# Down projection of a pair of tiles as seven products of two by two blocks, its bias as a matmul row, turned probabilities in place

## The chip, the core and the metric

The kernel runs on one core of a Trainium2 chip. The core has five engines that run side by side: TensorE (PE, with PEld for its weight loads), VectorE (DVE), ScalarE (ACT), GpSimd (POOL) and SyncE (SP, which issues most of the DMAs). Each takes its instructions in order and waits at semaphores for the others. SBUF is the on-chip memory, PSUM the memory that TensorE writes; this kernel uses PSUM as banks of 512 f32 columns. The metric is the device time of one execution in microseconds. All data and all matmuls are f32, unless said otherwise.

## What is computed

For x of 4096 tokens with 256 features the reference computes `x + attention_block(xn) + expert_block(xn)`, with xn the layer norm of x:

```python
# attention block: 8 heads, windows of 64 tokens, keys of the window before, the own and the next, band of 64
scores = einsum("bhcqd,bhckd->bhcqk", q, k3) * scale          # masked to the band
o = einsum("bhcqk,bhckd->bhcqd", softmax(scores), v3)
x = layernorm(x + o @ Wo + bo) * gamma + beta
x = x + gelu(x @ W1 + b1) @ W2 + b2
# expert block: 8 experts, two for each token, weights comb from the softmax of the gate's logits
h = silu((xf @ gw.T + gb) * (xf @ uw.T + ub))                 # 816 hidden columns
y = sum over experts of comb[:, e] * (h @ dw.T + db)
```

The change is in `h @ dw.T + db`, the down projection of the experts, and in how the probabilities of the attention are kept.

## The kernel before

**Units.** The tokens of each expert are gathered into tiles of 128. A unit is a pair of tiles (256 tokens) or a single tile of one expert. Thirty-four units always run: thirty pairs, with singles as units 3, 7, 11 and 15. Five more run only where the routing needs them; these go through `whole`, and the change leaves their down projection as it is.

**A step.** A loop over b = 0 to 33 does, in one step, gate and up of unit b, down of unit b-1 and, for b below 32 (`STEPS`), the attention of two tiles of queries (i, i+1) and one half of the heads (hq). An even b has hq 0. The order on every engine is that of the program (`manual_schedule`): nothing is reordered later. In a step TensorE does, in this order: the scores; the rest part of down (`down_rest`, L908); chunks 0 and 1 of gate/up; in even steps the output projection of the two tiles before (`closing`); the main part of down (`results`, L891); the transposes of the next unit's tokens (`turned`); up to b = 16 one share of keys, values or queries for later tiles; chunk 2; the transposes of the first half of the probabilities (`flip`, L1018, tile pT); chunk 3; those of the second half; two transposes for the keys that two tiles have in common (`flip_rest`, L1031, tile pX); chunk 4; the rest of gate/up; chunk 5; the products of probabilities and values (`weigh`, L1040).

**The probabilities.** VectorE reduces the scores against the mask into `pr` (L962). ScalarE takes the exponentials (L977). GpSimd, for each of four heads, adds the two halves of `pr` (L989) and multiplies the second half with an identity (L990); `apart` (L997) has it prepare `xd` before. In `scale`, VectorE takes the reciprocal of the sums (L1007), scales the first halves (L1009, waits for the last L989), reduces the second halves (L1010, waits for the last L990) and multiplies the result (L1011), for which GpSimd's L1013 waits. After `flip`, two VectorE operations (L1022) multiply the turned probabilities with a mask each, the first into a buffer of its own (`prT`), the second into the free half of `pr`.

**The experts' hidden columns.** 816 columns are six chunks of 128 (`FCM`) and 48 more (`REM`). A chunk is four matmuls, a ScalarE operation for the gate (L841) and a VectorE operation (L842) into `hT`, 128 hidden columns by tokens; silu (L874) follows for two chunks at a time. The 48 columns of the pair's first tile stand in rows 0 to 47 of chunk 6, those of the second in rows 64 to 111; the other rows of chunk 6 are zero.

**Down.** For each tile one matmul over the rows of chunk 6 (L884) and six over the chunks (L895), each of 128 hidden columns with 256 output columns, sum into one PSUM bank per tile (pe). VectorE then adds the bias, which the DMA of the weights `wd` has brought once per partition (256 columns), and writes y (L905); SP stores y (L918), and behind it in SP's queue issue the next loads of `wd` and, later, `wg`.

**Banks.** Seven banks of PSUM are handed out in the order of the program; a matmul into a new bank waits for whoever last read it.

Of the kernel before, what the change touches and what calls it, by code (L numbers as in the profile page):

```python
# [32 lines left out]
F32 = mybir.dt.float32  # L33
# [3 lines left out]
ALU = mybir.AluOpType  # L37
# [4 lines left out]
P = 128  # L42
# [12 lines left out]

REM = FE % P
REM_UP = P // 2
FM = FE - REM  # L60
FCM = FM // P
NT = S // P
G = 512
NG = S // G
# [24 lines left out]

GW, UW, RW, BW = 0, DC * FM, 2 * DC * FM, 2 * DC * FM + DC * P  # L90
GU = BW + 2 * FCM + 1
DN = FCE * D + D
HQ = 4
AHEAD = 4
WARM = 56
# [6 lines left out]
def block_kernel(ctx: ExitStack, tc: tile.TileContext, a: dict, out: bass.AP):  # L102
# [116 lines left out]

    att = ctx.enter_context(ExitStack())  # L220
    wqkv = pool(att, "wqkv", right)
    mask = wqkv.tile([P, 4, 2 * P], F32, tag="mask", name="mask")

# [87 lines left out]
    def make_mask():  # L311

        nc.gpsimd.memset(mask, 0.0)
        for kind in range(4):

            def keep(base, step, channel, m=mask[:, kind, :]):
                nc.gpsimd.affine_select(
                    out=m,  # L320
                    in_=m,
                    compare_op=ALU.is_ge,
                    fill=MASKED,
                    base=base,
                    pattern=[[step, 2 * P]],
                    channel_multiplier=channel,
                )

            keep(0, 1, -1)
            keep(2 * WIN, -1, 1)  # L330
            if kind == 0:
                keep(-WIN, 1, 0)
            if kind == 3:
# [539 lines left out]
    def silu(hT, lo, hi, on=slice(0, P)):  # L873
        nc.scalar.activation(hT[on, lo:hi, :], hT[on, lo:hi, :], AF.Silu)  # L874

    def silu_rest(hT):

        silu(hT, FCM, FCE, slice(0, REM_UP + REM if hT.shape[2] > P else REM))

    def results_rest(pds, w, hT):  # L880
        for t, pd in enumerate(pds):

            half = slice(t * REM_UP, (t + 1) * REM_UP) if len(pds) > 1 else slice(0, P)
            nc.tensor.matmul(  # L884
                pd,
                hT[half, FCM, t * P : (t + 1) * P],
                w[half, FCM * D : FCE * D],
                start=True,
                stop=False,
            )  # L890

    def results(pds, w, hT):
        for t, pd in enumerate(pds):
            for f in range(FCM):
                nc.tensor.matmul(  # L895
                    pd,
                    hT[:, f, t * P : (t + 1) * P],
                    w[:, f * D : (f + 1) * D],
                    start=False,
                    stop=(f == FCM - 1),  # L900
                )

    def summed(y, pds, w):
        for t, pd in enumerate(pds):
            nc.vector.tensor_tensor(y[:, t, :], pd, w[:, FCE * D :], ALU.add)  # L905
# [7 lines left out]
    def down(b, pds, w, hT):  # L913
        at, n, _ = UNITS[b]
        results(pds, w, hT)
        y = he.tile([P, TB, D], F32, tag="y", name=f"y{b}")[:, 0:n, :]
        summed(y, pds, w)
        nc.sync.dma_start(out=rows(done, at, n), in_=y)  # L918

    def whole(b, w, wd, xT, hT, banks, gss, y):  # L920

        _, n, _ = UNITS[b]
        n_in = n * P
        for k, f in enumerate([FCM] + list(range(FCM))):
            pb = halves(banks[k % 3])[:, :, 0:n_in]
            gs = gss[k % 3][:, 0:n_in]
            if f == FCM:
                rest_of(w, xT, hT, pb, gs)
            else:
# [8 lines left out]
        summed(y, pds, wd)  # L938

    def scores(i, hq):  # L940

        g = i // TG
        ps = [halves(bank(f"ps{i}_{hq}_{hh}")) for hh in range(HQ)]
        for j in range(2):
            lo = (i + j) % TG * P
            for hh in range(HQ):
                r = slice(hh * DH, (hh + 1) * DH)
                nc.tensor.matmul(  # L948
                    ps[hh][:, j, :],
                    qts[g][r, hq, lo : lo + P],  # L950
                    kts[g][r, hq, lo : lo + 2 * P],
                    start=True,
                    stop=True,
                )
        kind = 0 if i == 0 else 2 if i == NT - 2 else 1
        pr = sp.tile([P, HQ, 2, 2 * P], F32, tag="pr", name=f"pr{i}_{hq}", bufs=1)

        nm = sp.tile([P, 2, HQ], F32, tag="nm", name=f"nm{i}_{hq}")
        sums = sp.tile([P, 2, HQ], F32, tag="sums", name=f"sums{i}_{hq}")
        for hh in range(HQ):  # L960
            for j in range(2):
                nc.vector.tensor_tensor_reduce(  # L962
                    out=pr[:, hh, j, :],
                    in0=ps[hh][:, j, :],
                    in1=mask[:, kind + j, :],
                    scale=-1.0,
                    scalar=-LOWEST,
                    op0=ALU.add,
                    op1=ALU.min,
                    accum_out=nm[:, j, hh : hh + 1],  # L970
                )
        return pr, nm, sums
# [42 lines left out]
    def flip(i, hq, j, pr):  # L1015
        pb = bank(f"pT{i}_{hq}_{j}")
        for hh in range(HQ):
            nc.tensor.transpose(pb[:, hh * P : (hh + 1) * P], pr[:, hh, j, 0:P], ident)  # L1018

        prT = [sp.tile([P, HQ, P], F32, tag="prT", name=f"prT{i}_{hq}_{j}"), pr[:, :, j, P:]]  # L1020
        for t, m in zip(prT, (first_keys, second_keys)):
            nc.vector.tensor_tensor(  # L1022
                t, pb.rearrange("p (h q) -> p h q", h=HQ), bcast(m, HQ, 1), ALU.mult
            )
        return prT
# [204 lines left out]
    hTs = [he.tile([P, FCE, B], F32, tag=f"hT{k}", name=f"hT{k}", bufs=1) for k in range(2)]  # L1230
    for k in range(2):
        nc.gpsimd.memset(hTs[k][:, FCM, :], 0.0)
    res = {0: residual(0)}
    xT = {}
    pos, oTs = {}, {}
# [11 lines left out]
    for b in range(ALWAYS):  # L1247
# [7 lines left out]

        if b + 2 < ALWAYS:
            xs[b + 2] = gather(b + 2)
        if attends:
            pr, nm, sums = scores(i, hq)
            xd = apart(i, hq)  # L1260
        if 0 < b < STEPS:
            pds = down_rest(b - 1, downs[b - 1], hTs[(b - 1) % 2])
        if b == 0:
            xT[0] = turned(0, xs.pop(0))
        if attends:
            exps(pr, nm, sums, 0, 3)
            merge(pr, 0)
        chunk(0)
        if b >= STEPS:
            pds = down_rest(b - 1, downs[b - 1], hTs[(b - 1) % 2])  # L1270
            down(b - 1, pds, downs.pop(b - 1), hTs[(b - 1) % 2])
        if attends:
            exps(pr, nm, sums, 3, 6)
            merge(pr, 1)
# [5 lines left out]
        if hq == 0 and i - 2 in res:  # L1280
            closing(i - 2, oTs.pop(i - 2), res.pop(i - 2))
            if i < STEPS:
                res[i] = residual(i)
        if attends:
            scale(i, hq, pr, sums, xd)
        if b == STEPS:
# [16 lines left out]
        if b == STEPS + 1:  # L1303
# [2 lines left out]
            nc.vector.scalar_tensor_tensor(shift2, mv2[:, :, 0], -1.0, r2, ALU.mult, ALU.mult)  # L1306
            nc.vector.tensor_tensor(beta_b2, beta, b2, ALU.add)
            x2s[0] = second_loads(0)
        if 0 < b < STEPS:
            down(b - 1, pds, downs.pop(b - 1), hTs[(b - 1) % 2])  # L1310
        if b == ALWAYS - 1:
            load_unit(ALWAYS + 1)
        if b + 1 < ALWAYS:
# [58 lines left out]
    down(ALWAYS - 1, pds, downs.pop(ALWAYS - 1), last)  # L1372
    load_unit(ALWAYS + 2)
    for b in range(ALWAYS, BLOCKS):
        at, n, _ = UNITS[b]
# [139 lines left out]
```

## Time and profile before

| | |
|---|---|
| Time, median of 3 runs | 1083.43 us (1083.07 to 1084.13) |
| The profiled execution, its time | 1085.82 us |
| The same, span of its instructions | 1084.0 us |
| Granted TensorE clock, mean | 0.996 |
| Step of b = 17 (455.15 to 476.00) | 20.85 us: PE busy 20.85, DVE 13.25, ACT 12.25, POOL 10.14 |
| Step of b = 18 (476.00 to 498.58) | 22.58 us: PE busy 22.58, DVE 14.99, ACT 12.25, POOL 11.42 |
| Step of b = 11 (326.83 to 345.70) | 18.87 us: PE busy 18.87, DVE 13.06, ACT 10.33, POOL 10.15 |
| Seven products of the last stage (920.40 to 932.90) | 12.50 us: PE busy 12.50, DVE 8.42, ACT 3.40, POOL 0.12 |

The last four rows are busy times of each engine in a stretch of the span. An engine that is busy for the whole of a stretch doesn't wait in it. In lines of the time line, the first column is the start in microseconds from the span's start, the second the time of the group, then engine, line, operation, what it writes and reads, and how often; in brackets stands the idle time just before, with what ended it. Lines by group give the mean of one in nanoseconds; a matmul of f32 has two records, and the mean of a record is longer than the distance from one to the next, since matmuls are pipelined.

The steps are very regular. The first score matmuls of b = 17 to 31 follow each other by 20.85 us (odd b) and 22.58 us (even b), within 0.01, but for the last.

### The profile page before, as it was taken

How to read it: one execution, taken by the hardware profiler on the slowest of the kernel's cores; microseconds unless marked ns; L12 is line 12 of the kernel's file. 1: busy time of each engine (PE TensorE's matmuls, PEld its weight loads, DVE VectorE, ACT ScalarE, POOL GpSimd, SP SyncE). 2: the span in 40 equal slices, each digit the busy share in tenths (PEclk: the TensorE clock that was granted, in tenths of full speed). 3: DMA queues.
4: the chain of work that ended last, by engine and by line, in shares of the span. 5: the costliest groups of instructions: out<-in, count | busy, mean ns of one | idle time of the engine just before them, and what ended most of it. 6: DMA issues, size and time to landing. Idle time of an engine off the chain costs nothing. (4 is left out here: it accounts for less than half of the span.)

```text
span 1084.0 us, 19063 instructions
## 1 busy us (share of the span) xinstructions
PE 1071.3 (99%) x6808; PEld 858.0 (79%) x6808; DVE 656.5 (61%) x1707; ACT 527.0 (49%) x1226; POOL 452.7 (42%) x600
## 2 busy tenths in 40 slices
PE   8999999999999999999999999999999999999998
PEld 5677888887888788888888888888887847777778
DVE  6565657667666666766666766666533355555546
ACT  3536546555556545655565465556424363333320
POOL 5515544346444554455445544544520043222220
PEclk8999999999999999999999999999999999999999
DMA  8252435454445344644554445445576443333121
GB/s 284 74 204 84 161 128 190 138 186 147 147 163 184 134 150 153 214 147 139 183 185 143 164 158 190 157 135 187 163 246 229 157 146 110 97 98 96 60 63 40
DMA packets 61040, 163.42 MB, mean 151 GB/s; under 512 B 6576, under 2 KB 46896, under 8 KB 51472
## 3 DMA queue, kind: packets, MB, share of 16 engines
q1 hardware_dynamic: 54464, 144.48, 38.1%
q0 software_dynamic: 6480, 17.70, 6.0%
q8 instruction: 55, 0.90, 0.3%
q14 instruction: 41, 0.34, 0.1%
HBM read 140.28 MB, written 21.89 MB: 150 GB/s over the span
## 5 line engine op out<-in xcount | busy, mean ns | idle before, releaser
L833 PE MATMUL gu<-xsT,wg 128*128 128x256 f32 (+1 forms) x1632 | 362.5, 369 | 0.7 <-ACT xsT L825 0.7
L833 PEld LDWEIGHTS gu<-xsT,wg 128*128 128x128 f32 x1632 | 289.1, 190 | 45.3 <-DVE nm L962 8.6
L841 ACT ACTIVATE gs<-gu,wg 128x256 f32<-128x256 f32 (+1 forms) x204 | 92.4, 453 | 256.2 <-PE gu L833 253.3
L842 DVE SCALAR_TENSOR_TENSOR hT<-gu,wg,gs 128x256 f32<-128x256 f32 (+1 forms) x204 | 95.1, 467 | 174.2 <-ACT gs L841 174.0
L989 POOL TENSOR_TENSOR pr<-pr 128x256 f32<-128x256 f32 x128 | 93.0, 727 | 252.5 <-ACT pr L977 252.5
L895 PE MATMUL pe<-wd,hT 128*128 128x256 f32 x768 | 171.6, 379 | 0.0
L895 PEld LDWEIGHTS pe<-wd,hT 128*128 128x128 f32 x768 | 145.4, 190 | 20.5 <-issue 1.0
L1160 POOL DMA_INDIRECT got<-done,slot x64 | 64.3, 1004 | 176.9 <-DVE acc L1173 110.5
L990 POOL TENSOR_TENSOR pr<-pr,ident 128x256 f32<-128x256 f32 x128 | 126.2, 986 | 10.0
L977 ACT ACTIVATE pr<-pr,nm 128x256 f32<-128x256 f32 x256 | 126.7, 497 | 0.4
L1115 PE MATMUL ph<-x2T,W 128*128 128x512 f32 x256 | 111.4, 593 | 1.1 <-ACT x2T L1105 1.1
L962 DVE CUSTOM_DVE_ANT_0 pr<-ps,mask 128x256 f32<-128x256 f32 x256 | 90.7, 420 | 24.3 <-PE ps L948 24.3
L1122 ACT ACTIVATE hf<-ph,b 128x512 f32<-128x512 f32 x64 | 43.4, 688 | 118.3 <-issue 54.6
L874 ACT ACTIVATE hT<-hT 128x512 f32<-128x512 f32 (+3 forms) x148 | 80.8, 546 | 32.1 <-DVE hT L842 22.4
L1115 PEld LDWEIGHTS ph<-x2T,W 128*128 128x128 f32 x256 | 48.0, 190 | 58.9 <-issue 53.3
L807 POOL DMA_INDIRECT xs<-xnd,token x71 | 68.8, 969 | 49.7 <-DVE paired_tiles L774 32.3
L1009 DVE TENSOR_TENSOR pr<-pr,rec 128x1024 f32<-128x1024 f32 x32 | 39.2, 1225 | 27.5 <-POOL pr L989 27.5
L1196 DVE TENSOR_TENSOR acc<-u,acc 128x256 f32<-128x256 f32 x32 | 12.9, 423 | 70.1 <-ACT u L1199 69.6
L977 ACT ACT_TABLE_LOAD x31 | 39.8, 1283 | 23.5 <-DVE nm L962 23.4
L1010 DVE TENSOR_REDUCE same<-pr 128x8 f32<-128x1024 f32 x32 | 39.1, 1222 | 19.8 <-POOL pr L990 19.8
L977 ACT ACTIVATION_READ_ACCUMULATOR pr<-pr,nm 128x1 f32 x256 | 48.4, 189 | 0.0
L1186 PE MATMUL s<-V,hv 128*128 128x128 f32 x384 | 44.2, 275 | 0.0
(230 smaller groups left out, 1575.8 us busy)
## 6 DMA issues: line engine op xcount, KB each, us to landing
wg<-in_gate_up SPq DMA_DIRECT2D x37, 1670.5 KB, 7.0
wd<-in_down SPq DMA_DIRECT2D x37, 1024.0 KB, 5.6
done<-y SPq DMA_DIRECT2D x30, 256.0 KB, 2.2
x<-in_x SPq DMA_DIRECT2D x8, 512.0 KB, 5.4
xnd<-xn SPq DMA_DIRECT2D x8, 512.0 KB, 4.8
res<-xnd SPq DMA_DIRECT2D x16, 256.0 KB, 2.9
x1d<-res SPq DMA_DIRECT2D x16, 256.0 KB, 2.2
x<-x1d SPq DMA_DIRECT2D x8, 512.0 KB, 4.7
```

The lines of the kernel that those rows point to most:

```text
L807: nc.gpsimd.indirect_dma_start(out=x[:, t, :], out_offset=None, in_=xnd, in_offset=bass.IndirectOffsetOnAxis(ap=token[:, i : i + 1], axis=0),)
L833: nc.tensor.matmul(pb[:, k, :], w[:, lo : lo + P], xT[:, c, :], start=(c == 0), stop=(c == DC - 1),)
L841: nc.scalar.activation(gs, pb[:, 0, :], AF.Identity, bias=w[:, gb : gb + 1])
L842: nc.vector.scalar_tensor_tensor(hT[:, f, :], pb[:, 1, :], w[:, ub : ub + 1], gs, ALU.add, ALU.mult)
L874: nc.scalar.activation(hT[on, lo:hi, :], hT[on, lo:hi, :], AF.Silu)
L895: nc.tensor.matmul(pd, hT[:, f, t * P : (t + 1) * P], w[:, f * D : (f + 1) * D], start=False, stop=(f == FCM - 1),)
L962: nc.vector.tensor_tensor_reduce(out=pr[:, hh, j, :], in0=ps[hh][:, j, :], in1=mask[:, kind + j, :], scale=-1.0, scalar=-LOWEST, op0=ALU.a ...
L977: nc.scalar.activation(pr[:, hh, j, :], pr[:, hh, j, :], AF.Exp, bias=nm[:, j, hh : hh + 1], scale=-1.0, accum_out=sums[:, j, hh : hh + 1],)
L989: nc.gpsimd.tensor_tensor(first, first, second, ALU.add)
L990: nc.gpsimd.tensor_tensor(second, second, bcast(ident, 2, 1), ALU.mult)
L1115: nc.tensor.matmul(ph, W1[:, c, f * P : (f + 1) * P], x2T[:, c, :], start=(c == 0), stop=(c == DC - 1),)
L1160: nc.gpsimd.indirect_dma_start(out=y, out_offset=None, in_=done, in_offset=bass.IndirectOffsetOnAxis(ap=slot[:, k, i : i + 1], axis=0),)
```

## The change

**Down of a pair.** Hidden (256 tokens x 768) and weights (768 x 256) are taken as two by two blocks: a11, a12 are the even and odd chunks of the first tile, a21, a22 those of the second; b11, b12 are the even chunks with output columns 0 to 127 and 128 to 255, b21, b22 the odd ones. In place of eight block products there are seven, of sums of blocks (t1 = b12 - b11, t2 = b22 - t1, t3 = b22 - b12, t4 = b21 - t2, s1 = a21 + a22, s2 = s1 - a11, s3 = a11 - a21, and a12 - s2). A block product is three matmuls of 128 by 128 by 128. Single tiles keep `results`.

- `sums_of_down`: four GpSimd operations of 128x384 for t1 to t4; t1 takes the place of b12. They stand in GpSimd's order behind `apart` and ahead of the merges.
- `sums_of_experts_hidden`: three VectorE operations of 128x384 for s1 to s3; s3 takes the place of a21. They stand behind the reductions of the scores and ahead of chunk 0's L842.
- `results_of_pair`: the products, three into the tiles' own banks and four into a bank `shared`; between the first and the second product VectorE writes a12 - s2 in the place of a12. In VectorE's order this stands behind chunk 1 and `closing`, ahead of `scale`.
- `summed_of_pair`: ScalarE copies the shared bank into y; behind `scale`, VectorE adds within y (three operations) and adds the tiles' banks (two).

**Bias of down.** It is a row of the weights of chunk 6 now (rows 48 and 112), and the same rows of `hT` hold ones, which four GpSimd operations write ahead of the loop. silu leaves these rows out, so it is done for each tile apart. A single tile's rest matmul takes 64 rows in place of 128, and its VectorE operation is a copy.

**Turned probabilities.** The first of the two L1022 writes in the place of what was turned, in place of `prT`.

**Mask.** Its four kinds are three.

```diff
-DN = FCE * D + D
+DN = FCE * D
...
     def silu_rest(hT):
-        silu(hT, FCM, FCE, slice(0, REM_UP + REM if hT.shape[2] > P else REM))
+        for t in range(hT.shape[2] // P):
+            silu(hT[:, :, t * P : (t + 1) * P], FCM, FCE, slice(t * REM_UP, t * REM_UP + REM))
...
+    def sums_of_down(b, w):
+        ts = he.tile([P, 3, FCH, P], F32, tag="ts", name=f"ts{b}", bufs=1)
+        t2, t3, t4 = (ts[:, k] for k in range(3))
+        m = blocks_of_weights(w)
+        b11, b12, b21, b22 = m[:, 0, 0], m[:, 0, 1], m[:, 1, 0], m[:, 1, 1]
+        t1 = b12
+        for out_, left_, right_ in ((t3, b22, b12), (t1, b12, b11), (t2, b22, t1), (t4, b21, t2)):
+            nc.gpsimd.tensor_tensor(out_, left_, right_, ALU.subtract)
+        return ts
+
+    def sums_of_experts_hidden(b, hT):
+        ss = he.tile([P, 2, FCH, P], F32, tag="ss", name=f"ss{b}", bufs=1)
+        s1, s2 = (ss[:, k] for k in range(2))
+        m = blocks_of_hidden(hT)
+        a11, a12, a21, a22 = m[:, 0, 0], m[:, 0, 1], m[:, 1, 0], m[:, 1, 1]
+        nc.vector.tensor_tensor(s1, a21, a22, ALU.add)
+        nc.vector.tensor_tensor(s2, s1, a11, ALU.subtract)
+        nc.vector.tensor_tensor(a21, a11, a21, ALU.subtract)
+        return ss
+
+    def results_of_pair(b, pds, w, hT, ss, ts):
...
+        shared = bank(f"sh{b}").rearrange("p (k n) -> p k n", n=P)
+        product(pds[0][:, c1], n[:, 0, 1], m[:, 1, 0], stop=False)
+        nc.vector.tensor_tensor(n[:, 0, 1], n[:, 0, 1], ss[:, 1], ALU.subtract)
+        product(pds[1][:, c1], n[:, 1, 1], ts[:, 2])
+        product(shared[:, 0], n[:, 0, 0], m[:, 0, 0], True)
+        product(shared[:, 1], ss[:, 1], ts[:, 0], True)
+        product(shared[:, 2], n[:, 1, 0], ts[:, 1], True)
+        product(shared[:, 3], ss[:, 0], m[:, 0, 1], True)
+        product(pds[0][:, c2], n[:, 0, 1], m[:, 1, 1])
+        return shared
+
+    def summed_of_pair(y, pds, shared):
+        q = y.rearrange("p t (h n) -> p (t h) n", n=P)
+        nc.scalar.copy(q, shared)
+        yield
+        nc.vector.tensor_tensor(q[:, 1], q[:, 0], q[:, 1], ALU.add)
+        nc.vector.tensor_tensor(q[:, 2], q[:, 1], q[:, 2], ALU.add)
+        both = q.rearrange("p (t h) n -> p h t n", h=2)
+        nc.vector.tensor_tensor(both[:, 1], q[:, 1:3], bcast(q[:, 3], 2, 1), ALU.add)
         for t, pd in enumerate(pds):
-            nc.vector.tensor_tensor(y[:, t, :], pd, w[:, FCE * D :], ALU.add)
+            nc.vector.tensor_tensor(y[:, t, :], pd, y[:, t, :], ALU.add)
...
-        prT = [sp.tile([P, HQ, P], F32, tag="prT", name=f"prT{i}_{hq}_{j}"), pr[:, :, j, P:]]
+        prT = [pr[:, :, j, k * P : (k + 1) * P] for k in range(2)]
...
+        for behind in (REM, REM_UP + REM):
+            nc.gpsimd.tensor_tensor(
+                hTs[k][:, FCM, :],
+                hTs[k][:, FCM, :],
+                ident[:, behind : behind + 1].to_broadcast([P, B]),
+                ALU.add,
+            )
...
         if attends:
             pr, nm, sums = scores(i, hq)
             xd = apart(i, hq)
+        ts = sums_of_down(b - 1, downs[b - 1]) if b and UNITS[b - 1][1] > 1 else None
         if 0 < b < STEPS:
-            pds = down_rest(b - 1, downs[b - 1], hTs[(b - 1) % 2])
+            pds = down_rest(b - 1, downs[b - 1], before)
...
             exps(pr, nm, sums, 0, 3)
             merge(pr, 0)
+        ss = sums_of_experts_hidden(b - 1, before) if ts else None
         chunk(0)
...
+        made = iter(())
+        if 0 < b < STEPS:
+            made = down(b - 1, pds, downs.pop(b - 1), before, (ss, ts))
+            next(made)
         if attends:
             scale(i, hq, pr, sums, xd)
...
-        if 0 < b < STEPS:
-            down(b - 1, pds, downs.pop(b - 1), hTs[(b - 1) % 2])
+        list(made)
```

More of the change, by code (lines that the diff above doesn't have):

```diff
@@ L61 @@
 FCM = FM // P
+FCH = FCM // 2
 NT = S // P
@@ L221, in block_kernel @@
     wqkv = pool(att, "wqkv", right)
-    mask = wqkv.tile([P, 4, 2 * P], F32, tag="mask", name="mask")
+    mask = wqkv.tile([P, 3, 2 * P], F32, tag="mask", name="mask")
     first_keys = wqkv.tile([P, P], F32, tag="first_keys", name="first_keys")
@@ L315, in make_mask @@
         nc.gpsimd.memset(mask, 0.0)
-        for kind in range(4):
+        for kind in range(3):
             def keep(base, step, channel, m=mask[:, kind, :]):
@@ L332, in make_mask @@
                 keep(-WIN, 1, 0)
-            if kind == 3:
+            if kind == 2:
                 keep(2 * P - WIN - 1, -1, 0)
@@ L876, in silu_rest @@
     def silu_rest(hT):
-        silu(hT, FCM, FCE, slice(0, REM_UP + REM if hT.shape[2] > P else REM))
+        for t in range(hT.shape[2] // P):
+            silu(hT[:, :, t * P : (t + 1) * P], FCM, FCE, slice(t * REM_UP, t * REM_UP + REM))
     def results_rest(pds, w, hT):
         for t, pd in enumerate(pds):
-            half = slice(t * REM_UP, (t + 1) * REM_UP) if len(pds) > 1 else slice(0, P)
+            half = slice(t * REM_UP, (t + 1) * REM_UP)
             nc.tensor.matmul(
@@ L901, in results, with blocks_of_weights, blocks_of_hidden @@
                 )
-    def summed(y, pds, w):
+    def blocks_of_weights(w):
+        return w[:, 0 : FCM * D].rearrange("p (m e h n) -> p e h m n", e=2, h=2, n=P)
+    def blocks_of_hidden(hT):
+        return hT[:, 0:FCM, :].rearrange("p (m e) (t n) -> p t e m n", e=2, n=P)
+    def sums_of_down(b, w):
[7 more added lines that the diff above has]
+        return ts
@@ new lines, in sums_of_experts_hidden, with product @@
+    def sums_of_experts_hidden(b, hT):
[8 more added lines that the diff above has]
+    def results_of_pair(b, pds, w, hT, ss, ts):
+        n, m = blocks_of_hidden(hT), blocks_of_weights(w)
+        c1, c2 = slice(0, P), slice(P, D)
+        def product(to, left, right, start=False, stop=True):
+            for f in range(FCH):
+                nc.tensor.matmul(
+                    to,
+                    left[:, f, :],
+                    right[:, f, :],
+                    start=(start and f == 0),
+                    stop=(stop and f == FCH - 1),
+                )
[9 more added lines that the diff above has]
+        return shared
@@ L907, in down_rest, with summed @@
+    def summed(y, pds):
+        for t, pd in enumerate(pds):
+            nc.vector.tensor_copy(y[:, t, :], pd)
     def down_rest(b, w, hT):
@@ L911, in down_rest, with down @@
         return pds
-    def down(b, pds, w, hT):
+    def down(b, pds, w, hT, sums):
         at, n, _ = UNITS[b]
-        results(pds, w, hT)
         y = he.tile([P, TB, D], F32, tag="y", name=f"y{b}")[:, 0:n, :]
-        summed(y, pds, w)
+        if n > 1:
+            shared = results_of_pair(b, pds, w, hT, *sums)
+            yield from summed_of_pair(y, pds, shared)
+        else:
+            results(pds, w, hT)
+            yield
+            summed(y, pds)
         nc.sync.dma_start(out=rows(done, at, n), in_=y)
@@ L937, in whole @@
         results(pds, wd, hT)
-        summed(y, pds, wd)
+        summed(y, pds)
     def scores(i, hq):
@@ L954, in scores @@
                 )
-        kind = 0 if i == 0 else 2 if i == NT - 2 else 1
+        kinds = 0 if i == 0 else 1, 2 if i == NT - 2 else 1
         pr = sp.tile([P, HQ, 2, 2 * P], F32, tag="pr", name=f"pr{i}_{hq}", bufs=1)
@@ L964, in scores @@
                     in0=ps[hh][:, j, :],
-                    in1=mask[:, kind + j, :],
+                    in1=mask[:, kinds[j], :],
                     scale=-1.0,
@@ L1232, in block_kernel @@
         nc.gpsimd.memset(hTs[k][:, FCM, :], 0.0)
+        for behind in (REM, REM_UP + REM):
[4 more added lines that the diff above has]
+                ALU.add,
+            )
     res = {0: residual(0)}
@@ L1257, in block_kernel @@
             xs[b + 2] = gather(b + 2)
+        before = hTs[(b - 1) % 2][:, :, 0 : UNITS[b - 1][1] * P]
         if attends:
@@ L1267, in block_kernel @@
             merge(pr, 0)
+        ss = sums_of_experts_hidden(b - 1, before) if ts else None
         chunk(0)
         if b >= STEPS:
-            pds = down_rest(b - 1, downs[b - 1], hTs[(b - 1) % 2])
-            down(b - 1, pds, downs.pop(b - 1), hTs[(b - 1) % 2])
+            pds = down_rest(b - 1, downs[b - 1], before)
+            list(down(b - 1, pds, downs.pop(b - 1), before, (ss, ts)))
         if attends:
@@ L1308, in block_kernel @@
             x2s[0] = second_loads(0)
-        if 0 < b < STEPS:
-            down(b - 1, pds, downs.pop(b - 1), hTs[(b - 1) % 2])
+        list(made)
         if b == ALWAYS - 1:
@@ L1371, in block_kernel @@
     pds = down_rest(ALWAYS - 1, downs[ALWAYS - 1], last)
-    down(ALWAYS - 1, pds, downs.pop(ALWAYS - 1), last)
+    sums = None
+    if UNITS[ALWAYS - 1][1] > 1:
+        sums = (
+            sums_of_experts_hidden(ALWAYS - 1, last),
+            sums_of_down(ALWAYS - 1, downs[ALWAYS - 1]),
+        )
+    list(down(ALWAYS - 1, pds, downs.pop(ALWAYS - 1), last, sums))
     load_unit(ALWAYS + 2)
@@ L1447, in rows, with rest @@
         return m.reshape(E, -1, P, n).transpose(0, 2, 1, 3).reshape(E, P, -1)
-    def rest(up, gate):
+    def rest(up, gate, behind=0.0):
         m = np.zeros((E, P, up.shape[-1]), np.float32)
@@ L1453, in rest @@
         m[:, REM_UP : REM_UP + REM] = up[:, FM:]
+        m[:, REM] = m[:, REM_UP + REM] = behind
         return m
@@ L1472 @@
             rows(down[:, :FM], D),
-            rest(down, down),
-            np.broadcast_to(v["down_b"][:, None, :], (E, P, D)),
+            rest(down, down, v["down_b"]),
         ],
```

## The prediction

> **What bounds the kernel now.** I read the page's first part, then the chain of waits, then the time lines of one step.
>
> ```profile
> PE 1071.3 (99%) x6808; PEld 858.0 (79%) x6808; DVE 656.5 (61%) x1707; ACT 527.0 (49%) x1226; POOL 452.7 (42%) x600
> ```
>
> TensorE has almost no idle time, so every matmul removed is a gain as long as nothing makes TensorE wait. The profiled execution has a span of 1084.0 us and took 1085.8; the median shown is 1083.43, so I carry changes over in microseconds. The chain in order of time gives matmul prices free of overlap:
>
> ```profile
> 859.02 2.60 PE whole L895 x12
> ...
> 893.28 12.51 PE s L1186 x112
> ```
>
> Each f32 matmul has two records. 128x256: 2.60/12 = 0.217 us a record. 128x128 (the last stage, which already uses seven products): 12.51/112 = 0.112. Half the columns cost half.
>
> The change lies in steps b = 1 to 31 (one unit's gate/up beside half a head group of attention). One step of the late, tight kind (odd b from 17, step from 455.15; below, t is time from its first score matmul):
>
> ```profile
> 455.15 1.15 PE L948 MATMUL ps<-kt,qt 32*128 32x256 f32 x16
> ...
> 460.41 5.34 PE L895 MATMUL pe<-wd,hT 128*128 128x256 f32 x24
> 465.59 0.60 PE L820 MATMUL pts<-ident,xs 128*128 128x128 f32 x4
> 466.03 1.89 PE L833 MATMUL gu<-xsT,wg 128*128 128x256 f32 x8
> 467.76 0.60 PE L1018 MATMUL pT<-ident,pr 128*128 128x128 f32 x4
> ...
> 470.36 0.38 PE L1031 MATMUL pX<-ident,xd 128*128 128x128 f32 x2
> ```
>
> Down of the unit before stands at t = 5.26, the first turn of the probabilities (pT) at 12.61, pX at 15.21. VectorE in the same step:
>
> ```profile
> 462.91 0.20 DVE L1007 RECIPROCAL rec<-sums 128x8 f32<-128x8 f32 x1 [0.50 <-ACT pr L977]
> 464.51 1.23 DVE L1009 TENSOR_TENSOR pr<-pr,rec 128x1024 f32<-128x1024 f32 x1 [1.40 <-POOL pr L989]
> 466.36 1.22 DVE L1010 TENSOR_REDUCE same<-pr 128x8 f32<-128x1024 f32 x1 [0.62 <-POOL pr L990]
> 467.61 0.17 DVE L1011 TENSOR_TENSOR same<-same,rec 128x8 f32<-128x8 f32 x1
> 467.72 0.42 DVE L905 TENSOR_TENSOR y<-pe,wd 128x256 f32<-128x256 f32 x1
> ```
>
> and GpSimd, whose merges of the probabilities release L1009:
>
> ```profile
> 463.76 0.72 POOL L989 TENSOR_TENSOR pr<-pr 128x256 f32<-128x256 f32 x1
> 464.56 1.76 POOL L990 TENSOR_TENSOR pr<-pr,ident 128x256 f32<-128x256 f32 x1
> ```
>
> The reader is to see a second chain that is only just hidden: merges (t = 4.13 to 9.33, back to back), L1009 (to 10.59), the last L990, L1010, L1011, then y (12.57 to 13.3). From the order of instructions, pX takes the PSUM bank that the first y operation frees, and the matmuls behind it the bank of the second, in both kernels. Slack now: 2.0 us before pT, 2.2 before pX.
>
> **The change, part by part.**
>
> *Products.* Per pair 12 matmuls of 256 columns become 21 of 128: 24 x 0.217 = 5.20 becomes 42 x 0.112 = 4.69; saved 0.51 us. 30 pairs: -15.3 us at most. A rule speaks against it: the Trainium skill, "TensorE: Matmul & The Clock Gate", Back-to-back issue gap, gives 81 ns for a matmul of 128 columns with its weight load and 131 for 512, so short matmuls are dear. Estimate from it: 256 columns about 98 on a straight line, 128 then cost 0.83 of it, and the products 42 x 0.83 x 0.217 = 7.5 us, a loss of 2.3 us a pair (+70 us). The last stage's row (0.112, with a weight load for each) decides against the rule; only that row has the f32 form.
>
> *VectorE sums (ss, n12).* Three of 128x384 after the score reductions (which end at t = 4.0), a fourth after chunk 1's hT and in front of L1007. Nearest rows: 128x1024 from SBUF 1.22 us (L1146), 128x8 0.17 to 0.19; on the line between, 384 columns cost 0.57, 256 0.44, 128 0.31. VectorE itself is idle 0.94, 1.35 and 0.5 us there, so this 2.3 us hides for VectorE. But it delays GpSimd. Of 128 L990 the 32 that run beside L1009 take up to 1.77 us, the median 0.73: a VectorE operation with two SBUF inputs kept GpSimd out for 1.03 us of its 1.23. The new sums are of that kind, and fall on the merges. By the row 1.03/1024 of 384 columns = 0.39 each; 4 x 0.39 less 0.1 (the first starts before the merges) = 1.5 us. By the rule (the Trainium skill, "SBUF — State Buffer", Who interferes with whom: the later one blocks fully until the first finishes) 4 x 0.57 = 2.2. Below: 0, if they slip into gaps. I take the row, 1.5: the last L989 ends at 10.83, not 9.33. GpSimd in turn may hold up a sum; the fourth is needed by the last product, at 5.26 + 36 x 0.112 = 9.3, and should end by 8.8.
>
> *y.* Two VectorE operations become: 128, 128, 256 columns from SBUF, each dependent on the one before, then two with PSUM (0.42). In front of the first y's release stands 0.31 + 0.31 + 0.44 + three gaps of 0.03 = 1.15 us more; and GpSimd's xd (L1013, 0.62 us) is released at the same moment by L1011 and can hold the second back by 0.4. So the first y ends at 10.83 + (12.57 - 9.33) + 1.15 + 0.42 + 0.4 = 16.0, the second at 16.35 (now 13.0, 13.33). This is 3 us late at a place with 2.2 us of slack, and TensorE now comes 0.51 earlier.
>
> *GpSimd sums (ts).* Rows 128x128 0.457, 128x512 1.27: 384 columns 1.0, times 4 = 4.0 us after xd's two subtractions. Behind them queue the merges. GpSimd is idle 8.2 us there (L989 <- ACT), from t = -4.1; ts ends near 0.3, merges start at 4.1, product 2 needs ts at 5.9. Cover 3.8 us: nothing. Gone, it would be 1:1 into L1009.
>
> *ScalarE.* Copy of 128x512 (0.59, row vt) while it waits 5.1 us for chunk 2: nothing. silu_rest in two (2 x 0.31 for 0.42): off the path.
>
> *Edits at nothing.* Bias as matmul rows: no matmul more, wd loads 128 KB shorter on a queue that isn't waited for; y's SP DMA and, behind it, the next wd and wg issue 3 us later, needed some 20 us later. Turned probabilities in place: same operations; the next writer of pr waits for the same matmuls. Mask: fewer operations before the loop. Four GpSimd operations on hT before step 0, 3.1 us, where GpSimd has 3.12 us idle before its first merge: 0, at worst +0.5.
>
> **The sum, by kind of step** (pX or its equivalent arrives 0.51 earlier than now; first y at 16.0; 0.05 for a release):
> - Odd b, 17 to 31 (8): pX at 14.70 waits to 16.05, the next bank 0.12: 1.47 - 0.51 = +0.96 each, +7.7.
> - Even b, 18 to 30 (7): the output projection (1.73 us) puts pX at 16.42: no wait, -3.6.
> - b = 3, 7, 11, 15: the chunks are of one tile and two query copies (1.4 us) follow y on VectorE. Its run from y to the last turned product is unbroken (339.41 to 344.98), and the last weigh matmul has just 0.39 us of slack. y later by 3.0 and TensorE earlier by 0.51: the step grows by 3.0 - 0.4 = +2.6 each, +10.5.
> - b = 1, 5, 9, 13 (values, 1.73 us more TensorE): two waits of 0.1: -1.2 for four.
> - b = 2, 6, 10, 14: -2.0. b = 4, 8, 12, 16 turn a single tile: 0.
> - Three pairs behind step 31, without attention: -1.5, less 0.4 for the last one, whose first product now needs the last silu: -1.1.
>
> Sum +10.3: the profiled span would be 1094.3, the median **1094 us**.
>
> **Rivals.**
> - *Faster: GpSimd isn't held up.* If the sums cost the merges nothing and xd doesn't hold y, the first y ends at 14.1: no wait at pX, only b = 3, 7, 11, 15 lose 0.7 each. 23 x -0.51 + 2.8 - 1.1 = -10, 1073 to 1074. It needs a delay at y that stays under about 2.2 us where I have 3.0 (break-even: first y at 15.2). For it: L1009 is the only pair of the kind seen, and the merges leave gaps of 0.08. Against it: all 32 of these are slow.
> - *Slower still: the lock lasts for the whole instruction.* First y at 16.6: the twelve losing steps +0.6 each, values steps +2.6 together, even steps +1.7: +22, 1105.
> - *No change:* y near 15.2, 1083.
> - *The products aren't half the price* (the rule above), +70: the last stage's row is of the same form, I give it 0.02.
>
> **Chances.** Forecast 0.58 (1086 to 1100); lock for the whole instruction or DVE order worse 0.12; faster rival 0.25 (1073 to 1081); no change 0.05. The range 1074 to 1108 takes in all but the tails. A measurement of this kernel tells 0.2% (2.2 us) from no change: faster 0.25, same 0.05, slower 0.70.
>
> **What would show it.** Right: 42 product records a pair at 0.112; L989 of 0.73 stretched beside the sums, last merge at 10.8; first waits of TensorE in pX on y, 1 to 1.5 us in odd steps, none in even ones from 18; steps 20.85 -> 21.8, 22.58 -> 22.07, 18.87 -> 21.5. Wrong: merges at 0.73 throughout, or TensorE waiting for ts or in a product for n12.

## The result, and the profile after

| | before | after |
|---|---|---|
| Time, median of 4 runs each | 1083.25 us (1082.82 to 1084.13) | 1093.98 us (1093.06 to 1094.96) |
| Ratio | | 1.0094 (95%: 1.0082 to 1.0107) |
| Profiled execution: time, span, clock | 1085.82, 1084.0, 0.996 | 1094.96, 1093.0, 0.998 |
| First score matmul of step 0 (from the span's start) | 85.43 | 84.90 |
| Steps 0 to 31 | 694.64 | 702.08 (+7.44) |
| Steps 32, 33 and the last down | 45.53 | 46.80 (+1.27) |
| Units behind them that may be skipped (`whole`) | 37.36 | 38.45 (+1.09) |
| From there to the end of VectorE's last operation | 217.61 | 217.61 |

The kernel is slower by 0.9%, where 1094 us was forecast. The four stretches add up to +9.3 us (-0.53 + 7.44 + 1.27 + 1.09), against +9.0 in the span (what follows that last operation is 0.3 us shorter). The forecast sum was +10.3, but +11.4 of it lay in the steps and -1.1 behind them. So the total came out close partly because two errors cancelled.

The page's first part of the kernel after (busy time, share, instructions), to be held against the same line of before:

```profile
PE 1065.6 (97%) x7348; PEld 863.7 (79%) x7348; DVE 784.0 (72%) x1917; ACT 550.5 (50%) x1287; POOL 601.9 (55%) x722
```

TensorE has 5.7 us less to do and is idle 14.7 us more (27.4 of 1093.0, where it was 12.7 of 1084.0). The rest of the pair's work has gone to VectorE (+127 us) and GpSimd (+149 us). What TensorE waits for is in the view of waits, by waiting line and releaser: us in total, times, longest:

```profile
PE pX L1112 <- DVE y L977: 6.7, 8, 1.4
PE gu L835 <- DVE y L977: 5.7, 4, 1.4
...
PE gu L835 <- DVE xsT L827: 1.2, 1, 1.2
```

Neither of the first two exists before. Eight steps wait at pX (odd ones from 17) and four at gate/up (b = 3, 7, 11, 15). All twelve waits are for y.

The step of b = 17 begins at 460.42 in the kernel after (455.15 before). TensorE's time line there:

```profile
465.69 0.83 PE L948 MATMUL pe<-wd,hT 128*128 128x128 f32 x6
466.36 0.83 PE L948 MATMUL pe<-ts,hT 128*128 128x128 f32 x6
...
469.71 0.83 PE L948 MATMUL pe<-wd,hT 128*128 128x128 f32 x6
470.38 0.60 PE L822 MATMUL pts<-ident,xs 128*128 128x128 f32 x4
...
474.71 0.60 PE L1099 MATMUL pT<-ident,pr 128*128 128x128 f32 x4
476.06 0.41 PE L1112 MATMUL pX<-ident,xd 128*128 128x128 f32 x2 [0.75 <-DVE y L977]
476.31 1.99 PE L835 MATMUL gu<-xsT,wg 128*128 128x256 f32 x8
```

The products take 4.69 us from 465.69 to 470.38, 0.50 less than before (5.18 from 460.41 to 465.59). But pX, which would come at t = 14.71, stands at 15.64. The step is 21.41 us, 0.55 longer. GpSimd's time line of the same step:

```profile
464.56 0.93 POOL L1070 TENSOR_TENSOR pr<-pr 128x256 f32<-128x256 f32 x1 [3.12 <-ACT pr L1058]
465.56 0.93 POOL L1071 TENSOR_TENSOR pr<-pr,ident 128x256 f32<-128x256 f32 x1
466.45 1.04 POOL L1070 TENSOR_TENSOR pr<-pr 128x256 f32<-128x256 f32 x1
467.57 0.73 POOL L1071 TENSOR_TENSOR pr<-pr,ident 128x256 f32<-128x256 f32 x1
468.26 1.04 POOL L1070 TENSOR_TENSOR pr<-pr 128x256 f32<-128x256 f32 x1
...
470.06 0.73 POOL L1070 TENSOR_TENSOR pr<-pr 128x256 f32<-128x256 f32 x1
```

Four of the merges' operations take 0.93 to 1.04 us instead of 0.73. The last merge ends at 470.79 (t = 10.37, before 9.33). VectorE's time line shows what stood beside them, and the y chain that follows:

```profile
464.35 0.55 DVE L934 TENSOR_TENSOR ss<-hT 128x384 f32<-128x384 f32 x1
464.94 0.97 DVE L935 TENSOR_TENSOR ss<-ss,hT 128x384 f32<-128x384 f32 x1
465.82 1.08 DVE L936 TENSOR_TENSOR hT<-hT 128x384 f32<-128x384 f32 x1
...
467.62 1.10 DVE L958 TENSOR_TENSOR hT<-hT,ss 128x384 f32<-128x384 f32 x1
...
474.00 0.28 DVE L971 TENSOR_TENSOR y<-y 128x128 f32<-128x128 f32 x1
474.32 0.60 DVE L972 TENSOR_TENSOR y<-y 128x128 f32<-128x128 f32 x1
474.96 0.43 DVE L975 TENSOR_TENSOR y<-y 128x256 f32<-128x256 f32 x1
475.49 0.76 DVE L977 TENSOR_TENSOR y<-pe,y 128x256 f32<-128x256 f32 x2
```

The sum that begins ahead of the merges takes 0.55 us, those that begin while a merge runs take 0.97 to 1.10. Set the ends side by side, and the two engines are seen to take turns. The merge of 464.56 ends at 465.49; L935 began during it and ends 0.42 later, at 465.91. The merge of 465.56 began during L935 and ends 0.58 behind it, at 466.49; L936 ends 0.41 behind that merge, and the merge of 466.45 ends 0.59 behind L936. So of two operations that meet, the one that began first keeps its end, and all but about 0.14 us of the other (0.55 or 0.73 long when alone) comes after that end. This holds through the whole trace: 84 of VectorE's sums of 384 columns begin while a GpSimd operation runs, and end 0.41 to 0.42 us behind it, though their own times go from 0.56 to 1.65; 140 operations of the merges begin while a VectorE operation with both inputs in SBUF runs, and end 0.58 to 0.59 behind it (own times 0.92 to 1.77). Those that begin with the other side free take 0.55 to 0.56 and 0.72 to 0.74.

L972 takes 0.60 where L971 of the same size takes 0.28: GpSimd's xd (474.16 to 474.78) began before it. The first y ends near 475.9 (t = 15.5), and pX starts 0.15 behind it.

In b = 3, 7, 11, 15 the down stands 1.7 us earlier in the step. There TensorE also waits inside the products. TensorE's time line in b = 15 (from 418.60):

```profile
424.21 0.86 PE L948 MATMUL sh<-ts,ss 128*128 128x128 f32 x6
425.13 0.94 PE L948 MATMUL sh<-ts,hT 128*128 128x128 f32 x6
425.91 0.83 PE L948 MATMUL sh<-wd,ss 128*128 128x128 f32 x6
...
434.04 1.16 PE L835 MATMUL gu<-xsT,wg 128*128 128x128 f32 x8 [1.43 <-DVE y L977]
```

The products' starts should be 0.67 apart. Two of these distances are 0.92 and 0.78, so 0.36 of the 0.5 us gained is lost again. The product of 425.13 needs s3, which L936 finishes at 425.08; the products ahead of it are on time. Then 1.43 is spent waiting for y, and the step grows by 2.07.

### The profile page after: what moved, and what is told of

Same layout as the page of the kernel before. It is cut to its first block, busy times and chain, and to the rows that moved or that the text cites. A ratio compares the mean times of both kernels' runs of the same rounds, so it can differ in the third digit from the quotient of the medians.

```text
span 1093.0 us, 20590 instructions
## 1 busy us (share of the span) xinstructions
PE 1065.6 (97%) x7348; PEld 863.7 (79%) x7348; DVE 784.0 (72%) x1917; ACT 550.5 (50%) x1287; POOL 601.9 (55%) x722
## 5 line engine op out<-in xcount | busy, mean ns | idle before, releaser
L1070 POOL TENSOR_TENSOR pr<-pr 128x256 f32<-128x256 f32 x128 | 114.1, 892 | 135.3 <-ACT pr L1058 135.3
L1071 POOL TENSOR_TENSOR pr<-pr,ident 128x256 f32<-128x256 f32 x128 | 132.6, 1036 | 10.0
L844 DVE SCALAR_TENSOR_TENSOR hT<-gu,wg,gs 128x256 f32<-128x256 f32 (+1 forms) x204 | 91.5, 459 | 59.2 <-ACT gs L843 59.2
L876 ACT ACTIVATE hT<-hT 128x512 f32<-128x512 f32 (+2 forms) x179 | 85.2, 485 | 37.8 <-DVE hT L844 22.4
L1090 DVE TENSOR_TENSOR pr<-pr,rec 128x1024 f32<-128x1024 f32 x32 | 39.2, 1225 | 41.7 <-POOL pr L1070 41.7
L925 POOL TENSOR_TENSOR ts<-wd 128x384 f32<-128x384 f32 x60 | 60.2, 1003 | 3.4 <-issue 1.0
L969 ACT COPY y<-sh 128x512 f32<-128x512 f32 x30 | 17.6, 586 | 72.5 <-PE sh L948 72.5
L1091 DVE TENSOR_REDUCE same<-pr 128x8 f32<-128x1024 f32 x32 | 39.1, 1222 | 19.8 <-POOL pr L1071 19.8
L948 PE MATMUL pe<-wd,hT 128*128 128x128 f32 x360 | 50.6, 276 | 0.5 <-ACT hT L876 0.5
L948 PEld LDWEIGHTS pe<-wd,hT 128*128 128x128 f32 x360 | 46.8, 192 | 3.0 <-issue 1.0
```

The lines of the kernel that those rows point to most:

```text
L844: nc.vector.scalar_tensor_tensor(hT[:, f, :], pb[:, 1, :], w[:, ub : ub + 1], gs, ALU.add, ALU.mult)
L948: nc.tensor.matmul(to, left[:, f, :], right[:, f, :], start=(start and f == 0), stop=(stop and f == FCH - 1),)
L1070: nc.gpsimd.tensor_tensor(first, first, second, ALU.add)
L1071: nc.gpsimd.tensor_tensor(second, second, bcast(ident, 2, 1), ALU.mult)
```

## The experiments

Their chips ran the kernel before at 1085.62 us (22 runs, the first four kernels), 1085.84 us (11 runs, the next three) and 1084.5 us (one run, the last two). The absolute times in the expectations start from 1083.4, so the difference from before and the ratio are what to compare. "Step" below is a step's length against the same step of before.

**1. All edits but the products.** Pairs use `results` again; bias rows, turned probabilities in place and mask stay.

```diff
+SEVEN = frozenset()
-        if n > 1:
+        if b in SEVEN:
```

> Every pair keeps the old down projection (12 matmuls of 256 columns); bias as a matmul row, turned probabilities in place, mask of three kinds and silu of the 48 columns by tile stay. Theory (the 9 us come from the sums of the seven products alone): within 1 us of before, 1082.3 to 1084, no waits of TensorE in pX, last merge at t = 9.33. Rival (one of these edits costs, for instance the in-place probabilities or the four GpSimd operations ahead of the loop): 1086 or more.

Measured: 1088.52 us, ratio 1.0026 (1.0016 to 1.0037), +2.9 us. A miss: this kernel isn't within 1 us of the one before. Steps 1 to 30 are as before within 0.03 us, except that b = 4, 8, 12, 16 are +0.19 each. Step 31 is +1.89, step 0 +0.30, and the `whole` units +0.78. The +0.19 can be read from TensorE's time line. First before (step of b = 4), then this kernel:

```profile
169.25 0.70 PE L884 MATMUL pe<-wd,hT 128*128 128x256 f32 x2
169.78 3.62 PE L833 MATMUL gu<-xsT,wg 128*128 128x256 f32 x16
173.24 1.89 PE L1062 MATMUL wo<-Wo,oT 128*128 128x256 f32 x8
```

```profile
167.10 0.70 PE L886 MATMUL pe<-wd,hT 64*128 64x256 f32 x2
167.73 3.72 PE L836 MATMUL gu<-xsT,wg 128*128 128x256 f32 x16
171.28 1.89 PE L1144 MATMUL wo<-Wo,oT 128*128 128x256 f32 x8
```

The single tile's rest matmul has 64 rows instead of 128. To the group behind it are 0.63 us instead of 0.53, and that group takes 3.55 instead of 3.46 to the next. So half the rows cost 0.19 us more. The two single tiles among the `whole` units show the same (from the rest matmul to the next group 0.44 and 0.43 become 0.62 and 0.63, and the groups ahead of it and behind it are about 0.1 longer each), which makes their +0.78. In step 31 it is something else:

```profile
777.69 1.06 PE L1122 MATMUL po<-pr,vt 128*32 128x128 f32 x27
778.94 0.42 PE L1122 MATMUL po<-pr,vt 128*32 128x128 f32 x4 [0.19 <-issue]
780.39 0.27 PE L1122 MATMUL po<-pr,vt 128*32 128x128 f32 x1 [1.03 <-issue]
780.59 0.70 PE L836 MATMUL gu<-xsT,wg 128*128 128x256 f32 x2
781.80 1.46 PE L836 MATMUL gu<-xsT,wg 128*128 128x256 f32 x6 [0.51 <-issue]
```

Three gaps in TensorE, 1.73 us in sum, with no releaser that the profile shows. Runs 8 and 9 are about these.

**2. Without VectorE's sums.** s1 to s3 and a12 - s2 are left out, so what comes out is no longer the down projection; the run prices the operations only.

```diff
-        nc.vector.tensor_tensor(s1, a21, a22, ALU.add)
-        nc.vector.tensor_tensor(s2, s1, a11, ALU.subtract)
-        nc.vector.tensor_tensor(a21, a11, a21, ALU.subtract)
...
-        nc.vector.tensor_tensor(n[:, 0, 1], n[:, 0, 1], ss[:, 1], ALU.subtract)
```

> Leaves out the four VectorE operations of 128x384 (s1, s2, s3 and a12 - s2); the products read unsummed blocks in their place. Theory (these operations hold up GpSimd's merges, so y's bank is free too late): merges of 0.73 us again, last one ending at t = 9.33 in place of 10.36, second y at 14.8 in place of 15.83, no wait in pX in odd steps (20.35), b = 3, 7, 11, 15 still +1.1; 1077 to 1081. Rival (the longer chain of y operations alone makes y late): merges unchanged, 1092 to 1095. Rival (matmuls dearer than thought): stays above 1090 with no waits.

Measured: 1083.51 us, ratio 0.9981 (0.9972 to 0.9991), -2.1 us. GpSimd's time line, step of b = 17 (from 455.46):

```profile
462.58 0.73 POOL L1064 TENSOR_TENSOR pr<-pr 128x256 f32<-128x256 f32 x1
463.38 0.72 POOL L1065 TENSOR_TENSOR pr<-pr,ident 128x256 f32<-128x256 f32 x1
464.07 0.72 POOL L1064 TENSOR_TENSOR pr<-pr 128x256 f32<-128x256 f32 x1
```

The merges are back at 0.73 and the last ends at t = 9.33, as before. The second y ends at 14.80 instead of 15.83. pX doesn't wait, odd steps from 17 are -0.48, even ones -0.49, and b = 3, 7, 11, 15 still +1.17. So the sums delay the merges by 1.03 us, and this reaches y one to one. The gain falls just short of what was expected (-2.4 to -6.4 against 1083.4), because steps 32 and 33 with the last down took 2.8 us longer than before, 1.7 of it in three gaps like those of run 1, and step 31 still waited 0.4 us for y.

**3. Without the additions inside y.** Three VectorE operations behind `scale` are left out (L971, L972, L975).

> Leaves out the three VectorE additions within y (128, 128 and 256 columns); ScalarE's copy and the two additions from PSUM stay. Theory (y is late by the sum of two things, about 1.0 us of merges and 1.5 us of longer y chain, and either one alone would leave pX just in time): merges still end at 10.36, second y at 14.35, no wait in pX in odd steps, b = 3, 7, 11, 15 at +0.7; 1075 to 1080. Rival (only the merges matter, through L1009 and the first turn): steps as in the changed kernel, 1091 to 1094.

Measured: 1082.83 us, ratio 0.9970 (0.9959 to 0.9980), -2.8 us, less than the 3.4 to 8.4 expected. The second y ends at 14.37, so the chain is worth 1.46 us: 0.28, 0.60 and 0.43 and their gaps. Odd steps from 17 are -0.49, b = 3, 7, 11, 15 +0.60. Steps 0 to 31 are 7.8 us shorter than before, but the stretch behind is 6.3 us longer: products wait for the sums there (0.83 and 0.34 us at L935, 0.60 at L936), two gaps like those of run 1 add about 1 us, and the granted clock is 0.84 in 776 to 780 us and 0.74 in 780 to 784, where the kernel before has 1.00.

**4. Without GpSimd's sums.** t1 to t4 are left out; the products read blocks of the weights in their place.

> Leaves out GpSimd's four operations of 128x384 for t1 to t4; the products read unsummed weights in their place. Theory (they lie in GpSimd's idle stretch ahead of the merges, and only collide with VectorE at the end, in steps 31 and 33): steps 1 to 30 unchanged, the last steps 1.5 to 2.5 us shorter; 1091 to 1093. Rival (149 us more work on GpSimd is what makes the merges late): merges earlier, odd steps below 20.9, 1084 or less.

Measured: 1096.69 us, ratio 1.0093 (1.0077 to 1.0110), about the loss with them. Steps 1 to 30 are those of the changed kernel, so GpSimd's added load isn't what delays y in these. The total gain that was expected isn't there: the end grew. TensorE has three gaps of the kind of run 1 (0.45, 1.01, 0.33 from 785 us), and the granted clock is 0.93 on average in 780 to 830 us (the trace is of the slowest of the four runs). But one part of the expectation did come true, in step 31. The time line, first of the kernel after, then of this run:

```profile
779.22 1.05 POOL L925 TENSOR_TENSOR ts<-wd 128x384 f32<-128x384 f32 x1
...
779.44 1.10 DVE L975 TENSOR_TENSOR y<-y 128x256 f32<-128x256 f32 x1
...
781.22 0.41 PE L1112 MATMUL pX<-ident,xd 128*128 128x128 f32 x2 [1.43 <-DVE y L977]
```

```profile
777.75 0.43 DVE L971 TENSOR_TENSOR y<-y 128x256 f32<-128x256 f32 x1
...
778.86 0.41 PE L1108 MATMUL pX<-ident,xd 128*128 128x128 f32 x2 [0.76 <-DVE y L973]
```

In step 31 GpSimd's sums for the next step come right behind xd, and one of them begins ahead of the third addition of y (L975, here L971). Without them this addition takes 0.43 us instead of 1.10, and the wait at pX is that of the other odd steps.

**5. Seven products only where y was expected to be hidden.** Even steps and b = 1, 5, 9, 13: 15 pairs.

```diff
+SEVEN = frozenset(u for u in range(NT - 1) if UNITS[u][1] > 1
+    and ((u + 1) % 2 == 0 or (u + 1 < 16 and (u + 1) % 4 == 1)))
```

> Seven products only in the steps in which TensorE did not wait: even b (2, 6, 10, 14, 18 to 30) and b = 1, 5, 9, 13, fifteen pairs; all other pairs keep the old down projection. Theory (0.50 us of TensorE saved in each, and nothing given back): 15 x -0.5 and -0.5 from the start, about 1075.5, 1074.5 to 1077; odd late steps 20.85 again. Rival (the sums cost wherever they stand, by a steady overhead): 1081 or more.

Measured: 1081.85 us, ratio 0.9961 (0.9948 to 0.9974), -4.0 us. That is less than the 6.4 to 8.9 expected. Fourteen of the chosen steps are -0.49, but b = 1 is +0.08, as in the changed kernel: -6.8 in 15 steps. Of it 2.7 goes back in step 31 (+1.94, gaps again) and in the four single tiles (+0.77). The odd steps from 17 to 29 and b = 3, 7, 11, 15 are as before.

**6. y ahead of the reduction, pX behind chunk 4.** Same work, other order: on VectorE the y chain stands between L1090 and L1091 instead of behind L1092; on TensorE pX comes one gate/up chunk later.

```diff
         nc.vector.tensor_tensor(first, first, bcast(rec.rearrange(by_head), P, 3), ALU.mult)
+        list(made)
         nc.vector.tensor_reduce(same.rearrange(by_head), pr[:, :, :, P:], AX.X, ALU.add)
...
-            added = flip_rest(i, hq, xd)
         if b:
             chunk(4)
+        if attends:
+            added = flip_rest(i, hq, xd)
```

> All pairs by seven products; the five y additions stand between the scaling of the probabilities (L1090) and the reduction (L1091), where VectorE waits 0.6 us for GpSimd, and the two transposes of pX behind chunk 4. Theory (the cost is the late release of y's banks, not the work itself): first y at about 13.7, no wait in pX, odd steps 20.35; b = 3, 7, 11, 15 at about +1.2; 1079 to 1084. Rival (VectorE's total work is the bound of a step): odd steps stay at 21.3, 1090 or more.

Measured: 1081.52 us, ratio 0.9967 (0.9955 to 0.9980), -4.3 us. The merges are as slow as in the changed kernel (last one at 10.37), but the second y ends at 14.0 in odd steps from 17, and these are -0.49. That is ahead of 14.72, where pX stood in run 2, so there the earlier y alone would do. Step 31 is -0.49. b = 3, 7, 11, 15 are +1.57, a little more than expected.

**7. Both: that order, and eight products in b = 3, 7, 11, 15 and in the three last pairs.**

> The order of y and pX as in the run before it, seven products in all pairs up to step 31 but those of b = 3, 7, 11, 15, which have query copies on VectorE; these and the last three pairs keep the old down projection. Theory: 23 x -0.5 and -0.5 from the start, about 1071.5, 1070 to 1074. Rival (y between the two operations of scale delays the turned probabilities and so the next step): 1078 or more.

Measured: 1076.99 us, ratio 0.9919 (0.9906 to 0.9932), -8.9 us: faster than both kernels. Its waits of TensorE, from the longest on:

```profile
PE idle L549 <- POOL ident masks.py:199: 1.6, 1, 1.6
PE ptx L474 <- ACT xn L468: 1.2, 3, 0.9
PE ph L1198 <- ACT x2T L1188: 1.1, 2, 0.6
PE gu L836 <- issue: 1.0, 1, 1.0
```

No wait for y is left. 23 steps of 0.49 give -11.3, and 0.7 at the start is gained. Back go 0.77 in the single tiles, 0.35 in step 0, 1.37 in the stretch behind step 31 and 0.77 in the `whole` units. That is why it fell short of the 12 us expected.

**8 and 9. Run 1 with 32 matmuls fewer, and 32 more, ahead of all work** (`WARM = 24`, `WARM = 88`). They shift TensorE's stream of instructions.

> e1_rest_only with 32 of the 56 warming matmuls ahead of the kernel's work left out (they compute nothing that is used). In e1_rest_only TensorE stands for 1.73 us in the last step with attention, in three gaps 1.4 us apart (0.19, 1.03, 0.51, from 778.9, after 27 of the 32 records of L1122) whose end the profile puts down to 'issue'. Theory A, the gaps belong to a place in TensorE's stream of instructions (the next block of them comes late): they move to 32 records later, into the down after step 31 (some 15 records into L897, about 787 us), and stay about 1 to 1.7 us in sum unless the transfers beside them are weaker there. Theory B, they belong to what TensorE does there (a bank, an operand): same records as in e1_rest_only.

> e1_rest_only with 32 more warming matmuls (88 in place of 56). Theory A: the gaps move to 32 records earlier, to the third record of the last gu ahead of L1122, about 776.5 us; 1 to 1.7 us in sum, less if the transfers are weaker there. Theory B: same records as in e1_rest_only (the last five of L1122 and the gu behind).

Measured, one run each: 1087.64 and 1088.34 us. Neither theory's place. With 32 fewer the gaps are at the end of L1122 and the gu behind it (the group takes 1.43 instead of 1.08; then 0.52 and 0.73, at 780.8 and 782.2 us). With 32 more they are all in that gu (0.73 and 0.33 marked, at 781.7 and 783.2 us). They stay within about ten records, about 1.4 us apart, in a stretch where the DMA engines are busy 0.77 to 0.92 of the time. The Trainium skill ("Runtime: NRT & Kernel Launch", Instruction fetch mechanics) says that instructions come by DMA in blocks of 256, mostly hidden. The trace has one packet of such a queue at 772 to 774 us in run 1, at 778 to 780 with 32 fewer and at 766 to 768 with 32 more. The blocks moved by 6 us each way and the gaps did not. So it isn't that block. In run 1 VectorE also stood 3.6 us in that stretch for "issue". A second queue of that kind has a block at 778.4, 779.0 and 780.1 us in the three runs, just ahead of the gaps or among them, but in runs 2 to 5 and 7 none in the 15 us ahead of theirs. What the gaps are stays open; the changed kernel's own trace has none.

## Why the prediction was right, and where its sum was not

- *Products: right.* 42 records in 4.69 us, as worked out from the last stage's row; every step without a new wait is -0.49 (0.51 predicted). The rule of short matmuls (+70 us) doesn't hold for these f32 products.
- *VectorE sums: that they hold up the merges is right, the size is not.* The term "1.03/1024 of 384 columns = 0.39 each; 4 x 0.39 less 0.1 = 1.5 us" measures 1.03: 0.20 twice and 0.31 twice (0.93 - 0.73 and 1.04 - 0.73). Run 2 shows that it is the sums. Why it is less is in the lines of step 17: the engines take turns, and the one that begins second pays. In the row of L1009 VectorE began first (464.51 against 464.56), so GpSimd paid all, and L990 ends 0.58 behind L1009, as every merge does. Three of the four sums begin second. They pay 0.4 to 0.55 themselves, and the merge behind them, which begins about when the sum's own turn does, loses only what is left of it. The Trainium skill's rule ("SBUF — State Buffer", Who interferes with whom: the shared ports are an exclusive lock, and who issues first has them) agrees with this trace. The 2.2 us that the prediction took from it (4 x 0.57) let every sum begin first. So did the rival "the lock lasts for the whole instruction": its lock is what the trace shows, its 16.6 for y is not.
- *y chain: right.* From the last merge to the first y 5.17 us were predicted (10.83 to 16.0) and 5.1 measured (10.37 to 15.5). The hold by xd was there (L972 at 0.60, 0.32 for the 0.4 predicted). So the whole of y's error, 16.0 for 15.5, comes from the term above.
- *Steps.* With y 0.5 earlier each losing step loses less: odd ones +0.55 for +0.96, b = 3, 7, 11, 15 +2.07 for +2.6. The rest followed: even ones -0.49, b = 5, 9, 13 -0.49 and b = 1 +0.08 (for -1.2 in all four), b = 2, 6, 10, 14 -0.49. The note "wrong: TensorE waiting in a product" did come true in b = 3, 7, 11, 15, for 0.36 us, at the product that needs s3, not at n12.
- *"b = 4, 8, 12, 16 turn a single tile: 0": wrong,* +0.19 each. The halved rest matmul was counted as "no matmul more". Run 1 shows its price.
- *"Three pairs behind step 31: -1.1": wrong,* and so was +0.96 for step 31, which grew by 1.22. There GpSimd's sums meet VectorE's operations. In step 31 this is the L975 of run 4: 0.67 us more at pX, which is the difference to the other odd steps. The time line of the kernel after shows the y chain of step 32 and the sums of step 33:

```profile
794.37 0.99 POOL L925 TENSOR_TENSOR wd<-wd 128x384 f32<-128x384 f32 x1
794.48 1.03 DVE L971 TENSOR_TENSOR y<-y 128x128 f32<-128x128 f32 x1 [3.41 <-ACT y L969]
...
795.54 1.04 DVE L972 TENSOR_TENSOR y<-y 128x128 f32<-128x128 f32 x1
...
808.50 1.27 POOL L1221 TENSOR_TENSOR V<-W 128x512 f32<-128x512 f32 x1 [10.99 <-DVE ss L934]
808.54 1.65 DVE L935 TENSOR_TENSOR ss<-ss,hT 128x384 f32<-128x384 f32 x1
...
810.11 1.62 DVE L936 TENSOR_TENSOR hT<-hT 128x384 f32<-128x384 f32 x1
```

The same additions took 0.28 and (beside xd) 0.60 in step 17, and a sum with the other side free 0.55. GpSimd's L925 (four of 1.0 us, 793.3 to 797.5) and its sums for the last stage (L1221, 808.5 to 814.4) begin just ahead of them, and the turns are as above: L971 ends 0.15 behind the L925 shown, L935 0.42 behind the L1221. In these steps TensorE waits 0.4 us for s3, 1.2 for xsT and 0.5 for hidden. I had costed GpSimd's sums at nothing because it is idle 8.2 us there; that held for steps up to 30 (run 4 leaves them unchanged), but not where a VectorE operation comes at the same time. How much of +1.27 this is can't be said: run 4, without GpSimd's sums, has no wait for xsT, but another disturbance there.
- *The sum.* -4.0 us in steps 0 to 31 (+11.4 predicted, +7.4 measured) and +3.5 behind them (-1.1 for +1.27 and +1.09), with -0.5 at the start. That it came so close to 1094 is in part luck; its sign and the waits that it named are not.

## What to carry over

Seven products save TensorE 0.5 us a pair here, but the additions around them are paid on VectorE and GpSimd, and what counts is the one operation behind them that frees a bank. Before adding operations, ask whose memory accesses they stand beside, which of the two begins first, and how much slack the next release has: the same work placed ahead of a reduction, and left out in the few steps without slack, turned +0.9% into -0.8%. A stage with slack in its regular steps says nothing of its last steps; sum these apart.

## What was not expected of the hardware

- A VectorE operation with both inputs in SBUF and an operation of GpSimd took turns, and the second ended a fixed time behind the first, whatever their overlap: sums of 384 columns 0.41 to 0.42 us behind it, merges 0.58 to 0.60, in the kernel after and in runs 3, 4, 6 and 7 alike. So either engine can be the one that is slow, and a small operation can pay most: 128 columns took 1.03 us instead of 0.28 behind a GpSimd operation of 0.99.
- A single tile's rest matmul with 64 rows cost 0.10 us more than with 128 (0.63 for 0.53 to the next group), and the group behind it 0.09 more, though it does half the work.
- TensorE gaps of up to 1.03 us, about 1.4 us apart, without a releaser (runs 1 to 5 and 7 to 9, near 772 to 789 us), which moved by about ten records or less when 32 matmuls were added or left out ahead. Not explained.
